# Two-layer cross-attention on one core: row tiles for queries, keys and output sums in layer 0, and three kinds of transfer on ScalarE's queue

## The chip, the core and the metric

The kernel runs on one core of a Trainium2 chip. The core has a matrix engine (TensorE, PE in the profile), three engines for elementwise work (VectorE or DVE, ScalarE or ACT, GpSimd or POOL) and SyncE (SP), which here only issues transfers. An engine works through its own list of instructions in the order in which the program emitted them; engines wait for each other by semaphores. A transfer is issued by an instruction in the list of SP or ACT and then runs on 16 DMA engines. The metric is the device time in microseconds: the median of the runs shown.

## The reference

For each of four batch entries there are two attention layers over one context. All is float32.

```python
# layer 0: x (1024, 512), context (1024, 384), 16 heads of 64
h = layernorm(x) * gamma + beta
Q, K, V = h @ Wq, context @ Wk, context @ Wv
attn = softmax(Q K^T) * 64**-0.5          # per head, 1024 x 1024
x = x + (attn @ V) @ Wo + bo
# layer 1: 16 heads of 32
q, k = unit(rotate(rms(x) @ wq)), unit(rotate(context @ wk))
x = x + (softmax(q k^T * sqrt(32)) @ v) @ wout
```

## The kernel before

**Stages.** The batch loop has, for each entry b, the attention of layer 0, a short bridge (norm and first projections of layer 1), and the attention of layer 1. The 16 heads of layer 0 are taken as 8 pairs p of two heads; a pair has 8 query tiles i of 128 rows. So layer 0 is 64 **steps** (p, i) per entry, called step 0 to 63 below. Beside its own attention, a step also carries other matrix work.

**A step of layer 0** (`Attention0.step`) emits, in this order: the scores of the two heads (L368: four matmuls of 64 contraction rows, 128 columns of weights and 512 moving columns; the two heads use the upper and lower 64 rows of the array), row maxima on DVE (L393), exponentials on ACT (L394), then for the step before the transposes on DVE (L402), the scaling on GpSimd (L399), and at an even step the `regroup`: 16 transfers of 128 KB each on SP's queue (L413), which finish the transpose of the last two steps' probabilities. Two steps are a block. At an odd step, once two blocks wait, `product` multiplies the older block with the values (L429, result `av`). The first product is in step 5. Last comes `self.u.fill(us)`.

**Fill.** `Units` is a queue of small pieces of matrix work with a cost each. `fill(us)` runs pieces until their costs reach `us`; the batch loop works out `us` as all matrix work still to do, divided by the steps still to come, less the product's own cost. So the work is spread evenly by time. The pieces in layer 0 are, for the pair two ahead, the projections of keys (`pkT`, 6 pieces), queries (`pqT`, 8) and values (`pv`, 8), and the output sums (`po`, two pieces per tile: `vals` times `Wo`, added to `x` by DVE at L296). In the first two pairs the output sums are those left over from layer 1 of the entry before (the `tail`). In pairs 6 and 7 projections of layer 1 take the place of the pair projections.

**Array shapes.** All these pieces go through `matmul` (L166), which splits the 128 weight columns over two halves of the array: `128*64` in the profile, that is 128 rows and 64 columns, two at a time. The product is `128*64` as well. The scores are `64*128`. Each float32 matmul shows as two records on PE.

**Accumulators.** The program holds eight accumulators of 128 x 512, called banks here: four for scores (`s`, two tiles of two banks), four for the rest (`f0` to `f3`). `bank` hands out the four in turn. A bank is free again when ACT has copied it out (`evac`, L138) or DVE has added it to `x`.

**Transfers.** Besides regroups, SP's queue carries the weights of a pair (`pair_load`, L308, three transfers into one of two buffers `wpair`), the reload of `x` for the residual (`load_x`, L282, one tile at each even step of pairs 1 and 2, into one of 8 buffers that hold the `x` of the entry before until it is stored), the stores of the result (L868), the weights of layer 1 and the context. Only the pair weights of entry 0, pair 0 are on ACT's queue.

Of the kernel before, what the change touches and what calls it, by code (L numbers as in the profile page):

```python
# [94 lines left out]

def weave(chains, lag):

    res = []
    for i in range(len(chains) + lag):  # L100
        if i < len(chains):
            res += chains[i][0]
        if 0 < i <= len(chains):
            res += chains[i - 1][1]
        if i >= lag:
            res += chains[i - lag][2]
    return res
# [3 lines left out]
def xattn_kernel(ctx: ExitStack, tc: tile.TileContext, a: dict, out: bass.AP):  # L111
# [14 lines left out]
    which = {"n": 0, "from": 0, "cols": 2, "kept": None}  # L126

    def bank(name):

        while True:  # L130
            which["n"] = which["n"] + 1 if which["n"] < 3 else which["from"]
            if which["n"] != which["kept"]:
                break
            which["kept"] = None
        return ps_f.tile([P, 512], F32, tag=f"f{which['n']}", name=name)
# [37 lines left out]
    def context_units(b, ct):  # L173

        raws = {}

        def load(h):
            for t in range(4 * h, 4 * h + 4):
                if b == 0 and h:
                    raws[t] = sb.tile([P, S], F32, tag="vals", bufs=4, name=f"c_{b}_{t}")[:, :DC]  # L180
                else:
                    raws[t] = sb.tile([P, DC], F32, tag="row", bufs=4, name=f"c_{b}_{t}")
                nc.sync.dma_start(raws[t], c[b, t * P : (t + 1) * P, :])

        def turn_over(h, k):
            if k == 0:
                if h == 0:
                    both = sb.tile([P, NC_, S], F32, tag="ctxT", bufs=1, name=f"cT_{b}")
                    ct.extend([both[:, :, :512], both[:, :, 512:]])
            pp = bank(f"ptc_{b}_{h}_{k}")  # L190
            for t in range(4):
                nc.tensor.transpose(pp[:, t * P : (t + 1) * P], raws[4 * h + t][:, k * P : (k + 1) * P], ident)
            evac(ct[h][:, k, :], pp)

        return [
            {
                "load": [(0.0, lambda h=h: load(h))],
                "turn": [(0.45, lambda h=h, k=k: turn_over(h, k)) for k in range(NC_)],
            }
            for h in range(2)  # L200
        ]

    def norm_units(b, layer, hT, rows):
# [39 lines left out]
        def turn_over(h, k):  # L243
            if k == 0:
                hT.append(sb.tile([P, NQ, 512], F32, tag="hT", bufs=2, name=f"hT{layer}_{b}_{h}"))
            pp = bank(f"pth{layer}_{b}_{h}_{k}")
            for t in range(4):
                nc.tensor.transpose(pp[:, t * P : (t + 1) * P], got[h][t][:, k * P : (k + 1) * P], ident)  # L248
            if layer == 0:
                nc.scalar.activation(  # L250
                    hT[h][:, k, :], pp, AF.Identity, bias=cols[:, 1, k : k + 1], scale=cols[:, 0, k : k + 1]
                )
            else:
                nc.scalar.activation(hT[h][:, k, :], pp, AF.Copy, scale=cols[:, 2, k : k + 1])

# [24 lines left out]
    def load_x(b, xt, t):  # L280
        xt.append(sb.tile([P, DQ], F32, tag="x", bufs=8, name=f"x_{b}_{t}"))
        nc.sync.dma_start(xt[t], x[b, t * P : (t + 1) * P, :])  # L282
# [4 lines left out]
    def add_units(xt, lhs, w, name, cs, then=None):  # L287

        n = len(cs)

        def one(t, i, pp=[None]):
            if i == 0:
                pp[0] = bank(f"{name}_{t}")
            matmul(pp[0], lhs(cs[i])[:, t * P : (t + 1) * P], w(cs[i]), i == 0, i == n - 1)
            if i == n - 1:
                nc.vector.tensor_add(xt[t], xt[t], pp[0])  # L296
                if then is not None:
                    then(t)

        return [[(0.86, lambda t=t, i=i: one(t, i)) for i in range(n)] for t in range(NT)]  # L300


    def pair_load(b, p):
        w = sb.tile([P, NQ + 2 * NC_, P], F32, tag="wpair", bufs=2, name=f"w_{b}_{p}")
        f = slice(p * P, (p + 1) * P)
        eng = nc.scalar if (b, p) == (0, 0) else nc.sync
        for name, n0, n1 in (("Wk", NQ, NQ + NC_), ("Wq", 0, NQ), ("Wv", NQ + NC_, NQ + 2 * NC_)):
            eng.dma_start(w[:, n0:n1, :], a[name][:, f].rearrange("(n p) m -> p n m", p=P))  # L308
        return w

    def pair_units(b, p, w, hT, ct, res):
# [3 lines left out]
        def project(what, src, w0, nk, h, k, st={}):  # L315
            if what == "kT" and h == 0 and k == 0:
# [5 lines left out]
            if k < nk - 1:  # L322
                return
            if what == "qT":
                evac(res[what][:, h * 512 : (h + 1) * 512], st["pp"])
            else:
                quarters = res[what].rearrange("p (g c i) -> p c g i", g=4, i=32)
                evac(quarters[:, 4 * h : 4 * h + 4], st["pp"].rearrange("p (c g i) -> p c g i", g=4, i=32))

        def values(h, t, st={}):  # L330
            if h == 0 and t == 0:
                res["v"] = sb.tile([P, NT, P], F32, tag="v", bufs=3, name=f"v0_{n}")
            if t == 0:
                st["pp"] = bank(f"pv0_{n}_{h}")
            for k in range(NC_):
                matmul(
                    st["pp"][:, t * P : (t + 1) * P],
                    ct[h][:, k, t * P : (t + 1) * P],
                    w()[:, NQ + NC_ + k, :],
                    k == 0,  # L340
                    k == NC_ - 1,
                )
            if t == 3:
                evac(res["v"][:, 4 * h : 4 * h + 4, :].rearrange("p t f -> p (t f)"), st["pp"])
# [4 lines left out]
            "v": [(0.66, lambda h=h, t=t: values(h, t)) for h in range(2) for t in range(4)],  # L349
# [5 lines left out]
    class Attention0:  # L355


        def __init__(self, b, units):
            self.b, self.u = b, units
# [17 lines left out]
        def step(self, p, i, pr, us):  # L377
# [28 lines left out]
            self.u.fill(us)  # L406
# [14 lines left out]
        def product(self):  # L421
# [14 lines left out]
            evac(pr["vals"][:, q * W : (q + 1) * W], av[:, :W])  # L436

# [15 lines left out]
    def rotated_chains(dst, src, nk, w, name, tmp):  # L453
# [10 lines left out]
        def project(t0, i, k):  # L464
            if i == 0 and k == 0:
                tiles[t0] = [bank(f"{name}_p{t0}")]
                if which["from"] == 0:
# [8 lines left out]
        def rotate(t0, pp):  # L476
# [16 lines left out]
            tiles[t0] = t1  # L493

        def turn_over(t0):
# [9 lines left out]
            nc.scalar.copy(dst()[:, :, t0 * P : (t0 + TH) * P], pt.rearrange("p (g t) -> p g t", g=2))  # L505

# [30 lines left out]
    def value_chains(v, wv, ct, name):  # L537
        def one(t0, i, k, st={}):
# [5 lines left out]
            if i == TH - 1 and k == NC_ - 1:  # L544
                pv = st["pp"].rearrange("p (t g d) -> p g t d", t=TH, g=2)
                for g in range(2):
                    nc.scalar.copy(v[g][:, t0 : t0 + TH, :], pv[:, g])

# [139 lines left out]
    def prepare_units(b):  # L688

        st = {"ct": [], "hT": [], "pairs": [{} for _ in range(NPAIR)]}  # L690
# [5 lines left out]
        def project(p):  # L696
            def begin():
                if p + 1 < NPAIR:
                    w[p + 1] = pair_load(b, p + 1)

            begin = {"begin": [(0.0, begin)]}
            return begin | pair_units(b, p, lambda: w[p], st["hT"], st["ct"], st["pairs"][p])

        st["project"] = lambda p: flat(project(p).values())
# [50 lines left out]
    for b in range(B):  # L755
        ct, hT, pairs = st["ct"], st["hT"], st["pairs"]
        xt = []
        att = Attention0(b, work)
# [4 lines left out]
        for p in range(NPAIR):  # L763
# [7 lines left out]
            other = []  # L771
            if p < 2:
                other = tail[p * len(tail) // 2 : (p + 1) * len(tail) // 2]
            elif p % 2 == 0:
                i = p // 2 - 1
                outs = add_units(
# [6 lines left out]
                other = flat(outs[:4])  # L783
            else:
                other = flat(outs[4:])
            if p == 6:
                kq = {}
# [6 lines left out]
            if p == NPAIR - 1:  # L794
# [14 lines left out]
                other = k[2][0] + k[1][2] + flat(last)  # L809
                values = [(0.0, begin_v)] + vs[0][0] + k[3][0] + reload + k[2][2] + flat(c[0] for c in vs[1:]) + k[3][2]  # L810
            ahead = st["project"](p + 2) if p + 2 < NPAIR else []
            n = 7 * (p == 0)
            work.add(ahead[:n] + other)
            if p % 2 or other and p == 0:
                made[p + 1] = work.end()
            work.add(ahead[n:])
            if p + 2 < NPAIR:
                made[p + 2] = work.end()
            if p == 5:
                wq = []  # L820
                work.add([(0.0, lambda wq=wq: wq.append(half_q_load(0)))])
            left = sum(c for c, _ in values) if p == NPAIR - 1 else 0.0
            for i in range(NT):
                if b == 0 and p == 0 and i == 3:
                    work.until(begun)
                if left and i == 4:
                    work.add(values)
                    left = 0.0
                if 1 <= p <= 2 and i % 2 == 0:
# [3 lines left out]
                todo = work.total() + left + later + AV * ((NT * NPAIR + 1 - max(NT * p + i, 4)) // 2)  # L833
                att.step(p, i, pairs[p], max(todo / n - now, 0.0))
                if 2 <= p <= 3 and i < 2:
                    for t in range(2):
                        add_bo(xt, 4 * (p - 2) + 2 * i + t)
            if p + 1 < NPAIR:
                work.until(made[p + 1])
            else:  # L840
                work.drain()
            store_all()
# [8 lines left out]
        q = rotated_chains(lambda kq=kq: kq["q"], xnT, NQ, lambda k, wq=wq: wq[0][:, k, :], f"q1_{b}_0", tmp)  # L851
# [7 lines left out]
        which["from"], which["cols"] = 1, 4  # L859
# [7 lines left out]
        def store(t, b=b, xt=xt):  # L867
            stores.append(lambda: nc.sync.dma_start(out[b, t * P : (t + 1) * P, :], xt[t]))  # L868
# [58 lines left out]
        which["from"], which["cols"] = 0, 2  # L927
        if b == B - 1:
            tail = flat(adds[1][6:])
        else:  # L930
            outs = add_units(
                xt, lambda n, o=o: o[n], lambda n, w=wo1[1]: w[:, n % 2, :], f"po1_{b}_1", (2, 3), store
            )
            tail = flat(outs)
# [38 lines left out]
```

## Time and profile before

| | us |
|---|---|
| median of 3 runs | 2899.11 (2895.97 to 2902.00) |
| the profiled execution | 2892.38 |
| its span, first to last instruction | 2890.2 |
| layer 0, first to last score matmul, per entry | 432.9, 421.8, 422.1, 421.1 |
| bridge and layer 1, from one entry's last score of layer 0 to the next entry's first | 291.9, 291.9, 291.9 |

| engine | busy in the span | busy in layer 0 of entry 1 |
|---|---|---|
| PE | 98% | 420.2 of 421.8 us |
| DVE | 77% | 329.2 |
| ACT | 50% | 182.0 |
| POOL | 32% | 168.1 |

The granted clock of the matrix engine is 0.999 over the span. The DMA engines are busy for 77% of layer 0 of entry 1, at 178 GB/s. One regroup transfer keeps SP for 589 ns (the median of 2048), so the 16 of a block keep it for some ten of the thirteen microseconds of two steps.

The busy time of PE counts overlapping records and modelled ends, so 98% does not say that nothing is lost on it. The view to read is the chain of waits, which follows the work that ended last back to what released it, and lists for each piece where it starts and how long until the next.

### The profile page before, as it was taken

Reading aid. Unit: us, or ns where it says so; the run is one execution under the profiler, and the core shown is the slowest. Engines: PE = TensorE matmul, PEld = TensorE weight load, DVE = VectorE, ACT = ScalarE, POOL = GpSimd, SP = SyncE. Lnnn points to the kernel's source line nnn. Section 1 sums busy time; section 2 is a strip of 40 time slices with the busy share of each in tenths; the row PEclk is TensorE's granted clock in tenths of the full one; section 3 lists DMA queues with packets and bytes.
Section 4 is the critical chain, followed back from the end, with each engine's and each line's share of the span. In section 5 each row is a group of like instructions: output and inputs, shape, how many; then the busy total and the mean of one; then the engine's idle time right before and its main releaser. Section 6 shows DMA issues by size and latency. Waiting matters only on the chain.

```text
span 2890.2 us, 66288 instructions
## 1 busy us (share of the span) xinstructions
PE 2841.8 (98%) x27144; PEld 1423.0 (49%) x27144; DVE 2217.0 (77%) x2976; ACT 1436.6 (50%) x2308; POOL 938.9 (32%) x776
## 2 busy tenths in 40 slices
PE   8999999999999999999999999999999999999998
PEld 4444455555444444555544445455554445445544
DVE  5677786878777778687877777858887777785877
ACT  4443443666444444466644444446664444444664
POOL 2343344420134335332024333534102443353400
PEclk9999999999999999999999999999999999999999
DMA  5887775010388777401048887730105888772000
GB/s 142 192 186 181 167 171 138 22 36 26 77 208 191 185 169 173 118 22 37 26 96 212 191 185 166 175 97 22 36 26 124 208 189 190 164 172 74 2 2 31
DMA packets 177551, 348.84 MB, mean 121 GB/s; under 512 B 37601, under 2 KB 93153, under 8 KB 177249
## 3 DMA queue, kind: packets, MB, share of 16 engines
q1 hardware_dynamic: 175920, 343.96, 50.5%
q8 instruction: 214, 3.51, 0.5%
q14 instruction: 89, 0.72, 0.1%
q10 hardware_dynamic: 1328, 0.66, 0.1%
HBM read 67.64 MB, written 8.39 MB: 26 GB/s over the span
## 4 chain that ended last, share of the span: by engine, by line
PE 89%; DVE 4%; ACT 2%; issue 1%; DMA 1%; SPq 1%; POOL 1%; ACTq 0%; DVEq 0%
PE s L368 16%; PE av L429 15%; PE po L166 11%; PE s L586 9%; PE pv L166 8%; PE av L633 7%; PE pqT L166 7%; PE pkT L166 6%; PE q_p L166 4%; PE k_p L166 2%; PE av L669 1%; ACT e L596 1%; SPq L413 1%; DMA eT<-e 1%; PE pth L248 1%
## 5 line engine op out<-in xcount | busy, mean ns | idle before, releaser
L393 DVE TENSOR_REDUCE m<-s 128x1 f32<-128x1024 f32 x512 | 602.8, 1219 | 370.9 <-PE s L368 370.3
L596 ACT ACTIVATE e<-s 128x1024 f32<-128x1024 f32 x512 | 496.7, 1022 | 267.5 <-PE s L586 254.7
L368 PE MATMUL s<-qk 64*128 64x512 f32 x2048 | 518.8, 615 | 3.0 <-ACT e L394 2.2
L399 POOL TENSOR_SCALAR raw<-raw,li 128x1024 f32<-128x1024 f32 x256 | 287.1, 1122 | 722.3 <-DVE li L398 714.3
L394 ACT ACTIVATE e<-s,m 128x1024 f32<-128x1024 f32 x256 | 283.1, 1110 | 462.3 <-DVE m L393 238.9
L394 ACT ACTIVATE raw<-s,m 128x1024 f32<-128x1024 f32 x256 | 285.4, 1115 | 457.1 <-DVE m L393 456.9
L429 PE MATMUL av<-eT,v 128*64 128x256 f32 x4096 | 470.1, 382 | 4.4 <-DMA eT<-e 3.5
L399 POOL TENSOR_SCALAR e<-e,li 128x1024 f32<-128x1024 f32 x256 | 287.0, 1122 | 470.2 <-DVE li L398 237.0
L605 DVE TENSOR_TENSOR both<-e 128x512 f32<-128x512 f32 x512 | 340.9, 699 | 74.4 <-ACT e L596 72.3
L429 PEld LDWEIGHTS av<-eT,v 128*64 128x64 f32 x4096 | 285.2, 137 | 224.2 <-issue 84.6
L368 PEld LDWEIGHTS s<-qk 64*128 64x128 f32 x2048 | 184.6, 186 | 284.2 <-issue 167.9
L586 PE MATMUL s<-q,k 32*128 32x256 f32 x4096 | 306.7, 401 | 5.8 <-ACT q L505 2.7
L402 DVE STREAM_TRANSPOSE e<-e 128x1024 f32<-128x1024 f32 x256 | 310.0, 1228 | 0.3
L402 DVE STREAM_TRANSPOSE e<-raw 128x1024 f32<-128x1024 f32 x256 | 309.9, 1228 | 0.2 <-DMA eT<-e 0.2
L586 PEld LDWEIGHTS s<-q,k 32*128 32x128 f32 x4096 | 192.7, 184 | 141.0 <-ACT e L596 69.1
L166 PE MATMUL pqT<-hT,w 128*64 128x512 f32 (+1 forms) x1216 | 240.6, 595 | 2.5 <-ACT hT L250 2.5
L166 PE MATMUL po<-wo,vals 128*64 128x512 f32 x1024 | 234.6, 596 | 0.0
L296 DVE TENSOR_TENSOR x<-x,po 128x512 f32<-128x512 f32 x200 | 131.6, 678 | 84.9 <-PE po L166 84.2
L166 PEld LDWEIGHTS pv<-w,cT 128*64 128x64 f32 (+1 forms) x3360 | 170.3, 132 | 41.8 <-issue 34.1
L166 PE MATMUL pv<-w,cT 128*64 128x128 f32 (+1 forms) x3360 | 184.3, 274 | 0.9 <-ACT hT L250 0.7
L166 PE MATMUL pkT<-cT,w 128*64 128x512 f32 (+1 forms) x912 | 182.2, 597 | 0.0
L607 DVE TENSOR_TENSOR both<-both 128x1024 f32<-128x1024 f32 x128 | 159.7, 1248 | 4.4
(87 smaller groups left out, 2787.0 us busy)
## 6 DMA issues: line engine op xcount, KB each, us to landing
eT<-e SPq DMA_DIRECT2D x2048, 128.0 KB, 2.4
xr<-in_x_dram SPq DMA_DIRECT2D x32, 256.0 KB, 3.8
wo<-in_Wo_dram SPq DMA_DIRECT2D x16, 512.0 KB, 4.1
x<-in_x_dram SPq DMA_DIRECT2D x32, 256.0 KB, 4.2
out_dram<-x SPq DMA_DIRECT2D x32, 256.0 KB, 2.6
w<-in_Wq_dram SPq DMA_DIRECT2D x31, 256.0 KB, 3.2
c<-in_ctx_dram SPq DMA_DIRECT2D x32, 192.0 KB, 3.9
wkv<-in_wkv_dram SPq DMA_DIRECT2D x16, 384.0 KB, 3.3
```

The costliest lines, as they stand in the source:

```text
L166: nc.tensor.matmul(o[rr], lhsT[:, rr], rhs, start=start, stop=stop)
L368: nc.tensor.matmul(sc[j][:, kb * 512 : (kb + 1) * 512], pr["qT"][r[j], i * P : (i + 1) * P], pr["kT"][r[j], kb * 512 : (kb + 1) * 512], st ...
L393: nc.vector.tensor_reduce(m[:, j : j + 1], sc[j], AX.X, ALU.max, negate=True)
L394: nc.scalar.activation(e[j], sc[j].rearrange("p (g s) -> p g s", g=4), AF.Exp, bias=m[:, j : j + 1], accum_out=l[:, j : j + 1])
L399: nc.gpsimd.tensor_scalar(e[j], e[j], li[:, j : j + 1], HD0**-0.5, ALU.mult, ALU.mult)
L402: self.turn = [lambda j=j: nc.vector.transpose(self.e[:, :, i % BQ * 2 + j, :], e[j]) for j in range(2)]
L429: nc.tensor.matmul(av[r[j], :W].rearrange("p (t a i) -> p t a i", t=BQ, a=4), pr["v"][:, k, r[j]], eT[:, j, :, :, k * 32 : (k + 1) * 32], ...
L586: nc.tensor.matmul(sc[j // 2][:, j % 2, c, :], kT[rr, g, k * P : (k + 1) * P], qT[rr, g, qb * WQ : (qb + 1) * WQ], start=True, stop=True,)
L596: nc.scalar.activation(e, sc[u], AF.Exp, scale=float(np.sqrt(np.float32(HD1))))
L605: nc.vector.tensor_add(into[:, 2 * u : 2 * u + 2, :], es[u][:, :, 0, :], es[u][:, :, 1, :])
L607: nc.vector.tensor_add(acc, acc, into)
L633: nc.tensor.matmul(self.av[rr, 0, :], v[g][:, 2 * kk + c, rr], es[j // 2][:, j % 2, c, :], start=first and c == 0, stop=end and c == 1,)
```

## The change

Four things are changed together.

1. **Row tiles.** A `duo` computes two accumulators at once, with matmuls of 64 rows and 128 columns (the shape of the scores). It has two halves. In half 0 the upper 64 rows of the contraction go to the first bank and the lower 64 rows to the second; in half 1 they change places. Between the halves the two banks stay taken. Queries and keys of the pair two ahead are one duo each, and two tiles of output sums are one duo.
2. **Order.** While duos are there (`duos.begun`), an even step closes the open duo and opens the next, and does nothing else if one is open at both ends; an odd step runs one piece of the `Units` queue, or two when more than four are waiting. Values are now four pieces of two tiles each (cost 1.32), queued at i = 3, with a copy of 256 columns each. Entry 0 begins duos at step 8, the others at step 0; at step 16 of entry 0 and step 2 of the others no new duo is opened.
3. **Banks.** `bank` takes the one longest free from a list, and each user gives it back (`let_go`) after the copy or sum that empties it is emitted.
4. **Queues.** The loads of `x`, the stores of all entries but the last, and the pair weights (all but pairs 0 and 1 of entries 1 to 3) are issued by ACT. Pair weights are asked for at the next fill after the pair whose buffer they take has been projected. Loads of `x` are at odd steps, after all waiting stores have been issued at the even step before; `bo` is added at i = 3 and 5.

```diff
+class Duos:
+    SLOT = 0.86
...
+    def half(self, i):
+        n, f = self.open
+        f(i)
+        if i:
+            self.open = None
+        return n * self.SLOT
+
+    def fill(self, more):
+        us = self.half(1) if self.open else 0.0
+        if self.todo and more:
+            self.open = self.todo.popleft()
+            us += self.half(0)
+        return us
...
-        nc.sync.dma_start(xt[t], x[b, t * P : (t + 1) * P, :])
+        nc.scalar.dma_start(xt[t], x[b, t * P : (t + 1) * P, :])
...
+    def duo(names, n, lhsT, rhs, close):
+        pps = []
+        def half(i):
+            if i == 0:
+                pps.extend(bank(name) for name in names)
+            for k in range(n):
+                for t in range(2):
+                    o = t ^ i
+                    rr = slice(t * 64, (t + 1) * 64)
+                    nc.tensor.matmul(
+                        pps[o], lhsT(o, k)[rr], rhs(o, k)[rr], start=i == 0 and k == 0, stop=i == 1 and k == n - 1
+                    )
+            if i == 1:
+                for o in range(2):
+                    close(o, pps[o])
+                    let_go(pps[o])
+        return n, half
...
-        eng = nc.scalar if (b, p) == (0, 0) else nc.sync
+        eng = nc.sync if p in (0, 1) and b else nc.scalar
...
-            "v": [(0.66, lambda h=h, t=t: values(h, t)) for h in range(2) for t in range(4)],
+            "v": [(1.32, lambda h=h, t=t: values(h, t)) for h in range(2) for t in (0, 2)],
+            "duos": [project_duo("kT", ct, NQ, NC_), project_duo("qT", hT, 0, NQ)],
...
-            self.u.fill(us)
+            self.fill(i % BQ, us)
...
+            def then():
+                if 1 <= p < NPAIR - 2:
+                    st["due"].append(lambda: w.update({p + 2: pair_load(b, p + 2)}))
+                elif p == NPAIR - 2:
+                    st["due"].append(lambda: st["wq"].append(half_q_load(0)))
...
+        def fill(odd, us, b=b, duos=duos, st=st):
+            while st["due"]:
+                st["due"].popleft()()
+            if not duos.begun:
+                work.fill(us)
+            elif odd:
+                for _ in range(min(1 + (len(work.todo) > 4), len(work.todo))):
+                    work.one()
+            else:
+                alone = not duos.open
+                work.owed = us - duos.fill(duos.more)
+                if alone or not duos.open:
+                    work.fill(0.0)
...
+                ahead = st["project"](p + 2)
+                duos.add(ahead["duos"][:1] + sums[:1] + ahead["duos"][1:] + sums[1:])
...
+                if i == 3 and p < NPAIR - 2:
+                    work.add(ahead["v"])
...
+                if i % 2 == 0:
+                    store_all()
+                if 1 <= p <= 2 and i % 2:
                     load_x(b, xt, 4 * (p - 1) + i // 2)
...
+                duos.begun = duos.total() > 0 and NT * p + i >= (0 if b else NT)
+                duos.more = NT * p + i != (2 if b else 2 * NT)
...
-            stores.append(lambda: nc.sync.dma_start(out[b, t * P : (t + 1) * P, :], xt[t]))
+            eng = nc.sync if b == B - 1 else nc.scalar
+            stores.append(lambda: eng.dma_start(out[b, t * P : (t + 1) * P, :], xt[t]))
```

Here `sums` are two duos of output sums per pair: the `tail` of the entry before in pairs 0 and 1, and in pairs 2 to 5 those of heads already done. In pairs 6 and 7 the output sums stay pieces of the old shape. `lhsT` of a duo is, for keys and queries, the weights of the pair, and for sums the columns of `vals` of that tile.

## Prediction

> **What bounds the kernel.** On the page I read the busy time first, then the chain of waits. These lines are from the page:
>
> ```profile
> PE 2841.8 (98%) x27144; PEld 1423.0 (49%) x27144; DVE 2217.0 (77%) x2976; ACT 1436.6 (50%) x2308; POOL 938.9 (32%) x776
> PE 89%; DVE 4%; ACT 2%; issue 1%; DMA 1%; SPq 1%; POOL 1%; ACTq 0%; DVEq 0%
> eT<-e SPq DMA_DIRECT2D x2048, 128.0 KB, 2.4
> ```
>
> PE is the bound, and its share of the chain is larger still inside layer 0: the chain from 200 to 420 us holds nothing but PE. So what counts is PE's own time per piece. Some of that chain (start, us until the next piece, what):
>
> ```profile
> 297.52 1.72 PE pqT L166 x8
> 299.23 1.92 PE s L368 x8
> 301.15 4.44 PE pqT L166 x20
> 305.59 1.92 PE s L368 x8
> 307.51 3.60 PE av L429 x32
> 311.11 1.31 PE pv L166 x24
> ```
>
> Eight records of 512 columns cost 1.72 us behind a product (`pqT`), but 1.92 us as scores: 0.20 more. Twenty records behind scores take 4.44, where 20/8 x 1.72 is 4.30: 0.14 more. The 32 records of `av`, half as wide, cost 3.60 instead of 3.44. Taken record by record, two matmuls start together every 429 ns in either shape, `64*128` and `128*64`. Only at the change of shape does it differ: 0.10 before the first score slot, 0.10 in it, 0.10 before the first slot back, 0.05 in it. **A round trip costs 0.35 us**, and each of the 256 score groups makes one: 90 us.
>
> **Part 1: trips saved.** The arithmetic of a duo is that of the old pieces: halves of 3, 4 or 2 slots of 0.86 for keys, queries, sums. What goes is the way out and in around an even step that holds only scores and duo halves. I counted from the code which steps these are. The duos of a pair are keys, sums, queries, sums, and an even step closes one and opens one. In entries 1 to 3, step 0 opens keys alone and goes on to values; step 2 closes it (no new one is allowed) and goes on to values; step 4 opens a sum duo alone and values follow; steps 6 to 48 are pure; step 50 closes the last and layer-1 pieces follow: 22 pure steps. In entry 0, steps 10, 12, 14, 18 and 20 to 48 are pure: 19. Sum 3 x 22 + 19 = 85, times 0.351 = **-29.8 us**.
>
> A rule speaks against this part. The Trainium skill (TensorE: Matmul & The Clock Gate, Part 3, The mechanism) says that a weight load overlaps running matmuls only if it goes to other rows of the array. A duo uses the same two row halves all the time, so each slot would wait for its load. The weight loads of the scores at 305.52 (PEld is the load):
>
> ```profile
> 305.52 0.30 PEld L368 LDWEIGHTS s<-qk 64*128 64x128 f32 x4 [0.81 <-ACT qk L138]
> 306.06 0.19 PEld L368 LDWEIGHTS s<-qk 64*128 64x128 f32 x2 [0.24 <-issue]
> 306.49 0.19 PEld L368 LDWEIGHTS s<-qk 64*128 64x128 f32 x2 [0.23 <-issue]
> ```
>
> The later pairs of loads start with a slot of the same rows and end 0.19 us into its 0.43. By the rule the duos' 1,024 slots (264 in each of entries 1 to 3, 232 in entry 0) would each cost 0.187 more, +191 us; by the row nothing. I take the row.
>
> **Part 2: steps that become too short.** A step can't be shorter than its scores, maxima and exponentials, since the next scores need the same banks. ACT in the steps that start at 1028.48 and 1034.64:
>
> ```profile
> 1032.88 1.12 ACT L394 ACTIVATE raw<-s,m 128x1024 f32<-128x1024 f32 x1
> ...
> 1039.00 1.11 ACT L394 ACTIVATE e<-s,m 128x1024 f32<-128x1024 f32 x1
> ```
>
> They end 5.52 and 5.47 us after the step's start. In pair 7 of entry 1, steps reach this floor, and their scores take 2.14 and 2.18 instead of 1.92:
>
> ```profile
> 1141.15 2.14 PE s L368 x8
> 1143.29 3.60 PE av L429 x32
> 1146.89 2.18 PE s L368 x8
> ```
>
> So the floor is about 5.5. Before, the fill gave every step about the same work. After, an odd step gets one value piece (1.31), whatever it lacks. The first product is in step 5, so in entries 1 to 3 steps 1 and 3 have scores and one piece: 1.92 + 0.15 + 1.31 = 3.4, and PE waits 2.1 in each. (Four value pieces are waiting at step 0, which runs two, so step 1 gets one. At step 3 four new ones come in: one again, as "more than four" fails.) Step 4 then runs the other three, so steps 5, 7 and 9 have a product and no piece: about 5.3 to 5.5, of which I charge two with 0.25. That is 4.7 per entry. Entry 0 starts duos at step 8, with products there: two steps at 0.25. Sum **+14.6 us**. The work comes back nowhere: later steps get it at full price. Bounds: 0 if PE finds other work there, +16 if the five steps all end at 5.58, the latest exponential that I found.
>
> Later odd steps have 1.72 + 0.15 + 3.43 + 1.31 = 6.6, even ones 1.92 + 4.30 = 6.2 or 7.1: above the floor. Pairs 6 and 7 get what is left, about 85 of some 398 us of work over 14 steps, 6.4 a step with the trip; DVE, 83 to 85% busy there, allows it.
>
> **Part 3: DVE.** Both sums of a duo now fall together: 1.26 us for two, behind the second transpose, which ends 6.7 after the step's start. So DVE is free at 8.0. The shortest even step is 6.2 long and its successor's scores, without the way in, are ready 1.75 later, at 8.0. Nothing is lost; a further delay of DVE would first use up the 1.1 between an odd step's 6.6 and the floor. If that cover goes, each us costs one. I take 0.
>
> **Part 4: queues.** SP gives up about 130 issues of 0.4 to 0.6 us. It is not the bound, but 16 regroup issues of 0.59 hold it for some 10 us of a block's 13, and what stands ahead of them makes the product late: PE waited for regroups 2.69 us at 102, 0.81 at 851, 0.42 at 442 and 1564, 0.86 at 1618, the first two right where `x` loads were issued. The relief is 0 to 5.2; I take **-3**. ACT pays about 0.5 per issue (its three in this trace took 0.47 to 0.53). An `x` load stands before an odd step's exponentials, where ACT is idle 3.3 us and more; it waits for a store issued three steps earlier, and stores land in 2.6. A store waits for DVE's sum, which is done before the next maxima anyway. Pair weights, 1.5 us for three, stand behind the exponentials and before the copies of the duo, at 7.8 at the latest, when the product needs the bank at 8.1. In layer 1 the load for pair 2 adds 1.5 to a step of ACT with little room: +1 for three of them. Values copied in four parts instead of two cost ACT 4 x 0.37 - 2 x 0.58 = 0.3 per pair, beside idle time. At the start, 640 KB of weights for pair 1 now come among the first context and `x`, where the DMA engines are full until 18 us (350 GB/s): up to 1.8 late, of which the norm of `x` has 0.9 spare; **+1** (0 to 1.8).
>
> **Sum:** -29.8 + 14.6 - 3 + 1 + 1 = -16.2. The profiled execution took 2892.4 (span 2890.2), so its successor should take about 2876 (span 2874); the median of the runs is 6.7 above that execution, so **2883**.
>
> **Rivals.**
> - *Full gain, 2868.* The short steps cost nothing, as the planner or the banks shift work there. For it: `us` is worked out anew at every step. Against: an odd step doesn't read `us`. 2883 - 14.6.
> - *No start is free, 2909, slower.* The 0.10 by which a first score slot is stretched belongs not to the change of shape but to each new group of row tiles. A pure even step has three such starts (closing half, opening half, the next scores): 3 x 0.104 x 85 = 26.5 given back. For it: layer 0 never shows one row group right behind another. Against: groups in the column shape follow each other without a stretch, and are stretched only behind scores. It decides from 0.19 us per pure step, the point at which 16.2 are gone.
> - *Banks, 2915, slower.* The Trainium skill (TensorEngine Tiling, Gotcha 1: PSUM Pressure) says that row tiles need different banks and so raise the pressure on them; a duo holds two of four over two steps. By that, the opening half would wait for a copy of 0.38 at each pure step: +32. By the rows, it takes the banks of the last product and value piece, copied within 0.6 us of their end, and comes 3.6 us later at the earliest. I add nothing.
> - *Nothing to tell, around 2897:* more steps at the floor than counted eat the rest.
>
> **Chances.** Forecast (2876 to 2890) 0.56; full gain 0.17; still lower 0.02; nothing to tell 0.10; starts 0.10; banks, with regroups made late by ACT's queue, 0.05. A change of 0.2%, 5.8 us, can be told from none. So faster 0.75, within 0.10, slower 0.15. The range runs from the full gain with the whole relief of SP (2866) to the mild end of "starts" (2902).
>
> **What would show it.** In the chain of after, even steps of pairs 2 to 5 hold `s`, `pkT`, `pqT`, `po` at 0.86 per four records, and scores behind a duo take 1.72. If these take 1.8 or more, "starts" is right. In steps 1 and 3 of entries 1 to 3 the score piece should be preceded by some 2 us of DVE or ACT in the chain; if not, part 2 is wrong and the time is near 2868. A wait of PE for `qk`, `v` or `vals` copies before a duo half would show "banks"; waits of `av` for regroups would show that ACT's queue slows SP's.

## The result and the profile after

| | before | after |
|---|---|---|
| median | 2899.07 (2895.97 to 2902.00) | 2994.86 (2994.37 to 2995.94, 4 runs) |
| span of the profiled execution | 2890.2 | 2992.7 |
| granted clock over the span | 0.999 | 0.985 |

The ratio is 1.0329 (95% interval 1.0315 to 1.0343): slower by some 96 us, where 16 us of gain were forecast. On the page of after, the busy time, the first line of the chain of waits and the regroup's row of the transfers:

```profile
PE 2849.7 (95%) x27144; PEld 1528.2 (51%) x27144; DVE 2217.8 (74%) x2976; ACT 1445.0 (48%) x2372; POOL 936.9 (31%) x776
PE 79%; DVE 7%; DMA 6%; ACT 3%; SPq 2%; issue 2%; POOL 1%; ACTq 0%; DVEq 0%
eT<-e SPq DMA_DIRECT2D x2048, 128.0 KB, 2.4
```

PE's share of the chain fell from 89% to 79%, that of DMA rose from 1% to 6%. PE itself is busy for only 7.9 us longer, so the 102.5 us of the span are mostly waiting. The median landing of a regroup transfer is what it was. So these transfers are not slow as a rule; they are issued late, or the average hides a few. The waits say who stands (engine and line, waited for: us in total, times, longest). First PE, then, of SP's own list, the rows in which the line that issues the regroups waits for a transfer:

```profile
PE av L547 <- DMA eT<-e: 91.4, 25, 7.9
```

```profile
SPq L531 <- DMA w<-in_Wk_dram: 73.2, 16, 6.6
SPq L531 <- DMA out_dram<-x: 61.3, 17, 6.5
SPq L531 <- DMA w<-in_Wv_dram: 20.6, 7, 4.5
SPq L531 <- DMA x<-in_x_dram: 18.5, 14, 2.9
SPq L531 <- DMA eT<-e: 13.1, 13, 3.2
SPq L531 <- DMA w<-in_Wq_dram: 5.9, 11, 1.1
```

The product `av` waits 91.4 us for regroups. And SP, at the line that issues the regroups, waits 179.5 us (five of the six rows) for pair weights, stores and loads of `x`. A regroup reads and writes none of these. Before, the product waited 3.5 us, and such rows of SP came to 9.3 us, nearly all in the second line here:

```profile
PE av L429 <- DMA eT<-e: 3.5, 3, 2.5
SPq L413 <- DMA x<-in_x_dram: 8.3, 8, 2.7
```

The chain shows such a wait whole, in pair 2 of entry 1 (start, us, what):

```profile
899.34 1.08 ACT raw L512
...
900.47 0.44 ACT raw L512
...
900.94 3.03 DMA w<-in_Wq_dram
...
903.99 0.51 SPq L531
...
904.54 0.59 SPq L531
...
905.18 4.86 DMA eT<-e
...
910.27 5.07 PE av L547 x32
```

An exponential (L512) holds back ACT's issue of weights; these land; only then does SP issue (L531) a regroup transfer, which lands 4.86 later; the product starts 6.3 us late. ACT's own list in these microseconds:

```profile
900.47 1.11 ACT L512 ACTIVATE raw<-s,m 128x1024 f32<-128x1024 f32 x1
900.51 0.39 ACTq L392 DMA_DIRECT2D w<-in_Wk_dram  x1
900.94 0.50 ACTq L392 DMA_DIRECT2D w<-in_Wq_dram  x1
...
901.48 0.52 ACTq L392 DMA_DIRECT2D w<-in_Wv_dram  x1
903.37 0.36 ACTq L1019 DMA_DIRECT2D out_dram<-x  x1
903.77 0.63 ACTq L325 DMA_DIRECT2D x<-in_x_dram  x1
```

The three weight issues stand right behind the step's second exponential. They are the weights of pair 5, three pairs ahead, and nothing in this block needs them.

**Why SP waits for them** is in the compiled program of this case. Each transfer that SP or ACT issues signals one of eight completion semaphores, and its issue waits until the transfer that had this semaphore before it has landed. The turn of the eight goes over both queues together. It is fixed when the program is built, and isn't the order in which the kernel emits its transfers. Around the fence above the turn is, by semaphore:

```
6 Wk (ACT)   7 Wq (ACT)   0 regroup   1 Wv (ACT)   2 store (ACT)
3 regroup    4 x (ACT)    5 regroup   6 regroup    7 regroup
```

The last two regroup transfers are emitted before `Wk` and `Wq`, yet wait for them. In the whole program of after, 111 regroup transfers stand right behind a transfer of ACT on their semaphore (61 weights, 32 `x`, 18 stores), and 105 of those ACT transfers are emitted later than the regroup. With all transfers on SP's queue but the first three, the weights of entry 0, pair 0 (`rows_sp` below), there are none: there a transfer waits for one that was issued eight before it on the same queue and has mostly landed.

### The profile page after: what moved, and what is told of

The parts are those of the page before. It is cut to its first block, busy times and chain, and to the rows that moved or that the text cites. A ratio compares the mean times of both kernels' runs of the same rounds, so it can differ in the third digit from the quotient of the medians.

```text
span 2992.7 us, 66311 instructions
## 1 busy us (share of the span) xinstructions
PE 2849.7 (95%) x27144; PEld 1528.2 (51%) x27144; DVE 2217.8 (74%) x2976; ACT 1445.0 (48%) x2372; POOL 936.9 (31%) x776
## 4 chain that ended last, share of the span: by engine, by line
PE 79%; DVE 7%; DMA 6%; ACT 3%; SPq 2%; issue 2%; POOL 1%; ACTq 0%; DVEq 0%
PE av L547 15%; PE s L486 14%; PE s L708 8%; PE pv L207 7%; PE av L755 6%; PE po L207 5%; PE pqT L357 4%; PE q_p L207 4%; PE po L357 3%; DMA eT<-e 3%; PE pkT L357 3%; SPq L531 2%; PE k_p L207 2%; PE pqT L207 2%; DVE m L511 2%
## 5 line engine op out<-in xcount | busy, mean ns | idle before, releaser
L547 PE MATMUL av<-eT,v 128*64 128x256 f32 x4096 | 499.3, 399 | 94.6 <-DMA eT<-e 91.4
L512 ACT ACTIVATE e<-s,m 128x1024 f32<-128x1024 f32 x256 | 282.8, 1109 | 521.5 <-DVE m L511 205.2
L547 PEld LDWEIGHTS av<-eT,v 128*64 128x64 f32 x4096 | 308.7, 143 | 321.9 <-issue 193.0
L512 ACT ACTIVATE raw<-s,m 128x1024 f32<-128x1024 f32 x256 | 285.1, 1114 | 376.5 <-DVE m L511 376.3
L486 PEld LDWEIGHTS s<-qk 64*128 64x128 f32 x2048 | 196.2, 186 | 228.2 <-issue 173.0
L357 PE MATMUL pqT<-hT,w 64*128 64x512 f32 x768 | 173.2, 589 | 0.0
L755 PE MATMUL av<-e,v 128*32 128x256 f32 x2048 | 137.0, 385 | 0.0
L755 PE MATMUL av<-e,rest 128*32 128x256 f32 x2048 | 136.9, 385 | 0.0
L357 PE MATMUL pkT<-cT,w 64*128 64x512 f32 x576 | 134.3, 589 | 0.0
```

Of the source, the lines that this page charges most:

```text
L357: nc.tensor.matmul(pps[o], lhsT(o, k)[rr], rhs(o, k)[rr], start=i == 0 and k == 0, stop=i == 1 and k == n - 1)
L486: nc.tensor.matmul(sc[j][:, kb * 512 : (kb + 1) * 512], pr["qT"][r[j], i * P : (i + 1) * P], pr["kT"][r[j], kb * 512 : (kb + 1) * 512], st ...
L512: nc.scalar.activation(e[j], sc[j].rearrange("p (g s) -> p g s", g=4), AF.Exp, bias=m[:, j : j + 1], accum_out=l[:, j : j + 1])
L547: nc.tensor.matmul(av[r[j], :W].rearrange("p (t a i) -> p t a i", t=BQ, a=4), pr["v"][:, k, r[j]], eT[:, j, :, :, k * 32 : (k + 1) * 32], ...
L755: nc.tensor.matmul(self.av[rr, 0, :], v[g][:, 2 * kk + c, rr], es[j // 2][:, j % 2, c, :], start=first and c == 0, stop=end and c == 1,)
```

## The experiments

Two theories: **S**, the shared semaphores; and **B**, the bytes: weights, `x` and stores, moved at other times, slow the regroups. A third, **R**, was that the row tiles or their order are the loss; "no start is free" in the prediction is one form of it.

**Row tiles alone, and one kind of transfer at a time.** `rows_sp` takes all three edits of the queues back:

```diff
-        nc.scalar.dma_start(xt[t], x[b, t * P : (t + 1) * P, :])
+        nc.sync.dma_start(xt[t], x[b, t * P : (t + 1) * P, :])
-        eng = nc.sync if p in (0, 1) and b else nc.scalar
+        eng = nc.scalar if (b, p) == (0, 0) else nc.sync
-            eng = nc.sync if b == B - 1 else nc.scalar
+            eng = nc.sync
```

> The changed kernel with x loads, stores and pair weights back on SP's queue; row tiles and order as changed. S (shared semaphores: each transfer takes one of eight completion semaphores in turn, and is issued only when the one before it on that semaphore has landed, so SP's regroups wait for transfers that stand in ACT's list): no such waits are left, 2884 (2876 to 2895), the sum of the prediction without its queue terms; av waits for regroups fall from 91 us to under 10. B (bandwidth: ACT's transfers take DMA share from the regroups): the same 2884, or a few us more, since the bytes still move. R (row tiles or their order are the loss): about 2990, nothing comes back.

It took 2888.01 us, ratio 0.9956 (0.9940 to 0.9973). The loss is gone and a gain stays; R falls. The chain and the wait of the product for regroups:

```profile
PE 86%; DVE 6%; ACT 2%; SPq 2%; DMA 2%; issue 1%; POOL 1%; ACTq 0%; DVEq 0%
```

```profile
PE av L547 <- DMA eT<-e: 4.1, 3, 2.0
```

The view puts some waits of the product down to other names. All rows of `av` together are 12.3 us here, against 94.6 in after and 4.4 in before.

So everything lost, 2994.86 less 2888.01, some 107 us, comes with the queues. The next three take back two of the three edits each. `only_w` leaves the weights with ACT, `only_x` the loads of `x`, `only_st` the stores.

> As rows_sp, but the pair weights stay on ACT's queue. In the built program 69 regroup transfers come right after such a load on their semaphore. S: SP's waits for weights were 100 of 180 us in the changed kernel, so 100/180 of the 111 us of loss: 2946. B: weights are 54% of the 31.7 MB on ACT's queue: 2944. R: 2990. If neither holds it is at rows_sp.

> As rows_sp, but the x loads stay on ACT's queue; 27 regroup transfers come right after one on their semaphore. S: SP waited 18.5 us for them of 180: 2895. B: x is 26% of the bytes: 2913. R: 2990.

> As rows_sp, but the stores of entries 0 to 2 stay on ACT's queue; 24 regroup transfers come right after one on their semaphore. S: SP waited 61 us for them of 180: 2922. B: stores are 20% of the bytes: 2906. R: 2990. S has stores dearer than x loads, B cheaper.

| | us | ratio (95%) | over `rows_sp` | SP's waits for this kind |
|---|---|---|---|---|
| only_w | 2955.48 | 1.0187 (1.0167 to 1.0207) | 67 | 95 |
| only_x | 2917.79 | 1.0057 (1.0037 to 1.0077) | 30 | 55 |
| only_st | 2915.18 | 1.0054 (1.0034 to 1.0073) | 27 | 57 |

The longest row of SP's waits in each, in that order:

```profile
SPq L531 <- DMA w<-in_Wk_dram: 81.6, 19, 6.6
```

```profile
SPq L531 <- DMA x<-in_x_dram: 55.0, 21, 4.6
```

```profile
SPq L531 <- DMA out_dram<-x: 57.1, 14, 7.2
```

Each kind holds SP up by itself. The sizes don't decide between S and B, though. `only_x` is nearer to B's 2913 than to S's 2895, and the stores aren't dearer than the loads of `x`, as S had it: the 18.5 us that SP waits for `x` in after don't tell what `x` costs alone. The three sum to 124, not 107; that two kinds can share a wait would explain it, but wasn't tried.

**Transfers without bytes.** `tiny_act` is `rows_sp` with an extra transfer of 2 KB, into a tile that nothing reads, on ACT's queue beside each load of `x`, each transfer of pair weights (from pair 2 on) and each store that after has there (128 in all). `tiny_w` has it beside the pair weights only (72), and `tiny_pool` is that with GpSimd as the issuer.

```diff
+    def tiny():
+        d = sb.tile([P, NQ], F32, tag="tiny", bufs=8, name="tiny")
+        nc.scalar.dma_start(d, a["norm_w"])
...
+            if b or p > 1:
+                if p not in (0, 1):
+                    tiny()
```

> As rows_sp, all real transfers on SP, and beside each x load, each store of entries 0 to 2 and each pair-weight transfer from pair 2 on, a transfer of 2 KB into a tile that nobody reads, issued by ACT at that place. 96 regroup transfers come right after one of these on their semaphore (111 after an ACT transfer in the changed kernel). S: the bytes do not matter, the wait for a transfer that stands in ACT's list does: 2960 to 2995, SP's waits for these tiles 130 us and more. B: 128 transfers of 2 KB take no share of the DMA engines: 2888 as rows_sp, to 2892.

> As rows_sp, with a 2 KB transfer issued by ACT beside each pair-weight transfer of pairs 2 to 7 only; the weights themselves on SP. 66 regroup transfers come right after one of these on their semaphore (69 in only_w). S: all of only_w's loss of 67 us, 2955. B alone: 2888. If bytes and semaphores share the loss, as the 34 us of w_pool over rows_sp would have it: about 2920.

> As tiny_w, but the 2 KB transfers are issued by GpSimd. No regroup comes behind another queue's transfer on its semaphore, and no bytes move beside the regroups. If w_pool's 34 us are the weights' bytes on a second queue: 2888. If they are GpSimd's own issues (0.75 us each, 2.3 per pair) that hold up its scaling: about 2922.

`tiny_act` took 2961.44 us (1.0214, 1.0184 to 1.0244), 73 over `rows_sp`, with next to no bytes. Its rows of SP and of PE:

```profile
SPq L539 <- DMA tiny<-in_norm_w_dram: 118.0, 42, 5.6
```

```profile
PE av L555 <- DMA eT<-e: 46.6, 19, 4.1
```

SP waits 118 us for transfers that move nothing of use (S had 130 and more). B can't give that; S does. Nor do ACT's 128 more issues by themselves: PE waits 5.2 us for exponentials in layer 0, in `rows_sp` 5.0. `tiny_w` took 2940.28 (1.0138, 1.0102 to 1.0173), 52 over `rows_sp` where the real weights cost 67. The difference of 15 needn't be B: a transfer of 2 KB lands in 1.8 us (median), the weights in `only_w` in 2.7 to 3.6, so SP also waits longer for each. `tiny_pool` took 2884.54 (0.9944, 0.9925 to 0.9964): nothing lost. In the compiled program GpSimd's transfers use semaphores of their own, and no regroup stands behind one.

**The same bytes without the shared semaphores.** `w_pool` is `rows_sp` with the pair weights from pair 2 on issued by GpSimd.

```diff
-        eng = nc.scalar if (b, p) == (0, 0) else nc.sync
+        eng = nc.scalar if (b, p) == (0, 0) else nc.sync if p in (0, 1) else nc.gpsimd
```

> As only_w (2955), but the pair weights (pairs 2 to 7) are issued by GpSimd. In the built program GpSimd's transfers count on semaphores of their own, so no regroup comes behind a transfer of another queue on its semaphore. S: the 67 us of only_w over rows_sp go, but for what GpSimd's issues cost its scaling of the probabilities: 2888 to 2905. B: the same bytes still run beside the regroups on a second queue: 2945 and more.

It took 2922.50 (1.0080, 1.0055 to 1.0104), between the two theories. No regroup waits for weights now, but SP waits for its own earlier transfers, and PE for the regroups:

```profile
SPq L531 <- DMA eT<-e: 28.7, 38, 1.9
```

```profile
PE av L547 <- DMA eT<-e: 28.7, 13, 4.5
```

In its chain, regroup transfers take far more than the median of 2.4 to land, for example:

```profile
887.31 6.79 DMA eT<-e
...
941.87 6.74 DMA eT<-e
```

As `tiny_pool` is free and `w_pool` costs 34 over `rows_sp`, with as many issues, these 34 go with the bytes on a second queue. (An issue of weights keeps GpSimd for 0.74 to 0.80 us, one of 2 KB for 0.56; but GpSimd's share of the chain is 1%, as in `rows_sp`.) The Trainium skill (DMA: Bandwidth & Descriptors, Issuing engines are not separate DMA queues) says that several issuers save only the time of the issue, as all transfers share the 16 DMA engines; that agrees as far as it goes, but here SP is rid of 72 issues and the time is longer. So B isn't empty: it is the likely cause of the loss on GpSimd's queue, and on ACT's queue it can have at most the smaller part (15 of 67).

**Queues without row tiles.** `before_q` is the kernel before with the three edits of the queues, nothing else.

> The kernel before, with only the queues changed: x loads, stores of entries 0 to 2 and all pair weights but pairs 0 and 1 of entries 1 to 3 on ACT, at the places of the kernel before. 115 regroup transfers come right behind an ACT transfer on their semaphore. S: the loss does not need the row tiles: 2960 to 3010. R (the loss comes only with the row tiles or their order): 2899. The relief of SP that the prediction gave 3 us for would make it 2896.

It took 2946.78 (1.0163, 1.0137 to 1.0190): 48 lost against 107 with row tiles. The sign was expected, the size was missed. SP waits for weights, `x` and stores here too, in its line of regroups:

```profile
SPq L413 <- DMA w<-in_Wk_dram: 56.2, 15, 5.0
SPq L413 <- DMA x<-in_x_dram: 52.7, 24, 6.0
SPq L413 <- DMA out_dram<-x: 25.7, 16, 6.1
```

The built program has 115 such places, about as many as after. So their number doesn't tell the cost. The product waits 43.9 us for regroups in place of 91.4. Why the old order of steps takes it better wasn't tried.

**Asking earlier.** `w_early` is `only_w` with the pair weights asked for ahead of the step's scores, so that in ACT's list they stand before that step's exponentials.

```diff
         def fill(odd, us, b=b, duos=duos, st=st):
-            while st["due"]:
-                st["due"].popleft()()
...
+                while st["due"]:
+                    st["due"].popleft()()
                 att.step(p, i, pairs[p], max(todo / n - now, 0.0))
```

> As only_w, with the pair weights asked for at the start of the next step instead of behind its exponentials: they stand in front of them in ACT's list, some 3 to 5 us earlier. S: SP waits that much less for each load; of the 5.3 us by which steps 11, 19, 27 and 35 are too long in only_w, most go: 2900 to 2925. B: the same bytes at nearly the same time: 2955.

It took 2923.02 (1.0079, 1.0047 to 1.0111), 32 less than `only_w` and 35 more than `rows_sp`, inside S's range: the place in ACT's list makes half of the loss. SP's largest row fell from 81.6 to this:

```profile
SPq L531 <- DMA w<-in_Wk_dram: 49.5, 14, 6.6
```

**Filling the short steps.** `rows_sp_full` is `rows_sp` in which an odd step without a product fills by time, as before, and the queries of pair 1, until then done in layer 1 of the entry before, come into steps 1 and 3.

```diff
-            if i % BQ and len(self.blocks) == 2:
+            made = i % BQ and len(self.blocks) == 2
+            if made:
...
-            if not duos.begun:
+            if not duos.begun or odd and not made:
...
-                    pairs[1]["begin"] + pairs[1]["k"] + pairs[1]["q"],
+                    pairs[1]["begin"] + pairs[1]["k"],
...
-            ), pairs[1]["v"]
+            ), pairs[1]["q"] + pairs[1]["v"]
```

> As rows_sp, with the short steps filled: an odd step without a product runs the queue by time, and the query projection of pair 1 of entries 1 to 3 (6.9 us) is left from layer 1 for steps 0 to 3. If the short steps cost the 4.2 us per entry that part 2 of the prediction has for steps 1 and 3: 2888 - 12.6 = 2875, clearly under before. If the planner or later waits take it back: 2888.

It took 2887.66 (0.9957, 0.9940 to 0.9975): no gain over `rows_sp`. Steps 0 to 4 did get cheaper, 35.0 us in place of 32.3 with 6.9 us more work in them. But layer 1 became only 4.7 us shorter, and step 11, in which the product comes late even in `rows_sp`, took 10.99, 8.74 and 12.06 us in entries 1 to 3 instead of 8.94, 8.28 and 11.07. The late step in `rows_sp` (its chain):

```profile
803.32 6.95 DMA eT<-e
...
813.46 4.30 DMA eT<-e
...
817.85 3.67 PE av L547 x32
```

Two regroup transfers take 6.95 and 4.30 to land, against a median of 2.4. The last run moves the loads of `x` from SP to GpSimd's queue on top (`full_x_pool`), to free SP there:

```diff
-        nc.sync.dma_start(xt[t], x[b, t * P : (t + 1) * P, :])
+        nc.gpsimd.dma_start(xt[t], x[b, t * P : (t + 1) * P, :])
```

> As rows_sp_full, with the x loads issued by GpSimd, whose transfers count on semaphores of their own. What rows_sp_full gained in steps 0 to 4 it gave back at step 11 of the entries (8.7 to 12.1 us instead of 6.7). If SP's list does that, with x loads and stores ahead of the regroups: 2888 - 8 = 2880. If it is the bytes that run beside the regroups there, whoever issues them: 2888 or more.

It took 2887.98 (0.9958, 0.9947 to 0.9970); step 11 still takes up to 14.23. That doesn't clear SP's issues: by `w_pool`, transfers on GpSimd's queue can cost time of their own, and SP waits 14.3 us for its own regroups here, in `rows_sp_full` 2.5. The bytes of `x` beside the regroups are left as a suspicion.

## Why the prediction was wrong

**Part 4 is the step that failed**: "The relief is 0 to 5.2; I take **-3**" and "+1" for ACT in layer 1. In their place stand some +107 us with the row tiles (+48 without). The working asked what an issue costs ACT (about 0.5, right: 0.36 to 0.63 in the fence above) and whether each moved transfer comes in time for its own reader (it does: no reader of `x` or of the weights waits for one). It took for granted that a regroup on SP's queue depends on its data and on SP alone. In the built program it also depends on a transfer on ACT's queue through a semaphore that the two share, and so on the exponentials ahead of that. No line of the kernel shows this wait, and the trace of before, with nearly all transfers on one queue, shows it for 9.3 us only; the built program would have shown it.

How the loss is made up: the waits of the product are 94.6 us, less 12.3 in `rows_sp`. Then 15 of the 128 products of layer 0 take 1.4 to 2.9 us longer than the others, 29.3 us together (in `rows_sp` one, 1.6). That is 110 of the 111.2 us between the profiled spans (2992.7 and 2881.5).

Part 4's other terms were small, as said. In after, the first score of entry 0 starts 1.6 us later (25.6 against 24.0; forecast +1), and bridge and layer 1 are no longer than before (292.9 us against 293.3, from the start of the last score to the next entry's first; forecast +1 for three).

**Part 1 holds.** After a late product, the chain of after is the one that was forecast:

```profile
930.83 1.92 PE s L486 x8
932.74 1.72 PE po L357 x8
934.46 3.43 PE pqT L357 x16
937.89 1.72 PE s L486 x8
939.61 3.60 PE av L547 x32
943.21 1.31 PE pv L207 x24
```

Eight records of a duo take 1.72, and so do the scores behind one. From one step's first score to the next one's, undisturbed even steps of entry 1 take 6.11 or 6.97 (forecast 6.2 or 7.1), odd ones 6.73 (6.6). With that "no start is free" falls. So does, for this case, the rule on weight loads: slots on the same row halves start 429 ns apart, as before, and the loads lie inside the slot before:

```profile
934.29 0.19 PEld L357 LDWEIGHTS pqT<-hT,w 64*128 64x128 f32 x2 [0.24 <-issue]
934.72 0.19 PEld L357 LDWEIGHTS pqT<-hT,w 64*128 64x128 f32 x2 [0.24 <-issue]
```

**Part 2 holds.** In entry 1, steps 1 and 3 last 4.6, and about 2.3 us are lost around the end of each (forecast 2.1): before step 4, PE stands idle for 1.15 us, and the scores and the duo half behind them then take 1.16 longer than undisturbed ones. So the wait falls partly into the next step, and the step itself ends before the floor of 5.5. The chain of `rows_sp` from step 3 to step 4:

```profile
763.94 1.97 PE s L486 x8
765.90 1.22 DVE m L511
...
767.21 1.21 ACT e L512 x2
...
768.46 2.65 PE s L486 x7
```

The next scores wait for maxima and exponentials, as was said. "Full gain" falls with it. Parts 1 and 2 together said -15.2; `rows_sp`, which is these two parts, gave -13.4 between the medians (2901.41, measured beside it, to 2888.01), -8.7 between the profiled spans. That the sum comes so near is partly luck: it holds a loss that neither part has. The product waits 7.9 us more than before (12.3 against 4.4), and one product is slow by 1.6. Step 11 stands out here: its excess over 6.73 is 8.1 us in entries 1 to 3. Without that the two parts would have given some 3 to 8 us more than forecast; to which of them these belong isn't shown.

**Part 3** stays at nothing: no wait for DVE takes the place of the trips in the undisturbed steps.

**The rivals.** "Banks" ended on the right side, with 0.05 for it. But its mechanism is wrong: PE has no wait for the copies of `qk`, `v` or `vals` in front of a duo. Only its addition "with regroups made late by ACT's queue" came true, and it had no price of its own. The sign to look for ("waits of `av` for regroups would show that ACT's queue slows SP's") was named and appeared. It deserved a rival of its own: a regroup is late by as much as ACT is, at each of the places where the queues meet.

**Open.** Why the build orders the turn of the semaphores as it does, why the old order of steps loses 48 and the new one 107, how the 34 us between `tiny_act` (73) and after (107) divide between longer landings, more places and bytes beside the regroups, and what exactly makes step 11 late. The best version found is `rows_sp` (with `rows_sp_full` and `full_x_pool` the same within their intervals): row tiles with all these transfers left on SP's queue.

## What to carry to other kernels

Moving transfers to a second issuing engine isn't free just because that engine has time: here issues of both queues share eight completion semaphores, and a transfer that nobody is waiting for can hold up one that everybody waits for. Before such a move, look in the built program for which transfer stands before which on a semaphore, and after it, read SP's own waits first: a row in which one transfer waits for another that has nothing to do with it is the sign. Change the queues and the arithmetic one at a time; the gain of 13 us was there and lay under the loss.

## What the hardware showed beyond that

**A late product is also a slow one.** PE in four stretches around the wait at 910 (start and end, length, busy us and records of each engine, granted clock, DMA share, GB/s); two of them:

```profile
910.00:914.00 4.00, 3.73 (x22) 2.51 (x24) 2.60 (x4) 2.30 (x4) 2.17 (x2) 0.61 0.94 208
930.00:960.00 30.00, 30.00 (x218) 16.24 (x216) 20.14 (x26) 12.09 (x23) 11.98 (x11) 1.00 0.74 173
```

Right behind the wait of 6.3 us the clock granted to PE is 0.61, and the product takes 5.07 in place of 3.60; twenty microseconds later the clock is 1.00. The Trainium skill (TensorE: Matmul & The Clock Gate, Part 1: The HAM clock gate) describes this: after some time without work the clock falls back and needs a stretch of work to return. So a stall of PE costs more than its length: the slow products, 29 us in after, come on top of the waiting. Not every wait has this price, and what decides isn't shown: the product at 969.68, behind a wait of 3.5 us, took 3.67, while in `before_q` one at 1627.22, behind a wait of 1.95 us, took 5.36.
